# Pairing 768 instead of 1024 keys of the mixed heads in a graph attention kernel

## Chip, cores and metric

One core of a Trainium2 chip runs the whole program. The metric is device time in microseconds, lower is better. PE is TensorE's matmuls, PEld its weight loads, DVE VectorE, ACT ScalarE, POOL GpSimd, SP the engine that issues most DMAs.

## What is computed

A layer of graph convolution (x, 3327 nodes by 128) is followed by an attention layer over all pairs of nodes, in 128 heads of 8 components. The attention is where the time goes:

```python
q = (x @ Wq.T).reshape(d, n, h)      # d = 128 heads, n = 3327 nodes, h = 8
k = (x @ Wk.T).reshape(d, n, h)
v = (x @ Wv.T).reshape(d, n, h)
a = jnp.einsum('dnh,dmh->dnm', q, k) * scale
a = a + adj + adj
a = jax.nn.softmax(a, axis=2)
out = jnp.einsum('dnm,dmh->dnh', a, v)
out = out.reshape(n, h * d)
return out @ Wo.T
```

A layer norm of x + out closes it. adj has about five entries a row; the kernel takes the dense softmax without adj and adds the few neighbours of a node apart, on POOL.

## The kernel before

**Three passes over the same products.** Heads are worked in 32 groups of GH = 4, and the queries of a group in seven blocks of 512 (the last has 255). For each head and query the kernel needs (a) the largest product over all 3327 keys, so that exp can't overflow, (b) exp of every product less that maximum, (c) the sums of exp times v. Products come from PE as bf16 parts: query and key rows are split in three bf16 parts, 48 rows in all. The parts lie twice in the tiles k_st and q_st: rows 0 to 49 for (b), with two more rows that add the negative maximum, and rows 64 to 111 for (a).

**(a) is a stream of items.** `items_of` lists, for each row tile i of 128 queries, thirteen items; `max_item` (L544) works one: two matmuls of 512 keys (L553) into the two banks of a PSUM tile m of 1024 columns (pool ps_m, two buffers), then DVE takes the maximum of a row into a slot of mx (L573). Two of the four heads (MIXED = 0 and 2) save DVE work by pairs: of two keys a and b the larger product is half the sum plus the size of half the difference, s + |d|. The stage before stores half sums and half differences of neighbouring keys in kk_d (`mixed_keys`, `store_mixed`), and `load_group` (L282) puts them into the key tile of the mixed heads. PAIRED = 1024 keys of each mixed head are paired: 512 differences and 512 sums. A mixed head has three items:

- "size": a bank of 512 half differences and a bank of 512 plain keys. ACT writes the sizes of the first (Abs, L563) to the tile size; DVE takes the maximum of the second. The two read different banks of one tile, and the code says so with declare_no_dep.
- "sums": a bank of 512 half sums and a bank of 512 plain keys. DVE adds sizes and sums and keeps the maximum in one instruction (L567, tile larger, followed by a read of its accumulator), then takes the maximum of the plain bank.
- a plain item of 1024 keys.

The head next to it has three plain items. So the thirteen are size, sums, plain, three plain, again for heads 2 and 3, and one item of tails, the last 255 keys of all four heads.

**The order is written out by hand** (manual_schedule from L696). An iteration of the main loop (L735 to L772) takes the next item of the stream and interleaves it with (b) and (c) of a block that is 76 items behind. Its order of issue: the item's first matmul (L553), the first e_ps matmul (L751; ps_e has three buffers), the item's second matmul, the second e_ps matmul, exp of the first bank on ACT (L761, es<-e_ps), Abs if the item is a size item, exp of the second bank, the item's DVE instructions, and then four products with v (L719) of two iterations back. There are 10816 iterations and as many items. At the ends of a block some products are bunched in 512 columns, and o_sb (L728) is copied out.

**Beside it**: after a block's last item DVE reduces the slots of mx to nm (L516), POOL splits it in two bf16 parts, DVE transposes them (L529, tile turned), and SP sends them to the queries' extra rows. Every fourth iteration the generator `neighbours` issues a step of the neighbours' part: gathers and products on POOL, some maxima on DVE (L655 to L660), exponentials on ACT (L667). SP's loads of the next group's keys and next block's queries are cut in pieces, and one piece is started with every second item (`begin_next`).

Of the kernel before, what the change touches and what calls it, by code (L numbers as in the profile page):

```python
# [9 lines left out]
F32 = mybir.dt.float32  # L10
# [3 lines left out]
AF = mybir.ActivationFunctionType  # L14
ALU = mybir.AluOpType
AX = mybir.AxisListType
# [4 lines left out]
P = 128  # L21
N = 3327
# [6 lines left out]
NB = 512  # L29
# [6 lines left out]
PARTS = 3  # L36
# [7 lines left out]
LOWEST = -3.0e38  # L44
MW = 1024
# [4 lines left out]
LEAD = 38  # L50
TURN = 8
MIXED = (0, 2)
PAIRED = MW
SLOTS_MX = 5


def paired_from(head):

    return -head * N % (2 * D)
# [7 lines left out]
def gnn_layers(ctx: ExitStack, tc: tile.TileContext, x, adj, adjt, w_in, w_out, wq, wk, wv, wo, out):  # L67


    nc = tc.nc  # L70
# [19 lines left out]
    kk_d = dram.tile([2 * PARTS * H, G // 2], BF16, name="kk_d")  # L90
# [31 lines left out]
    with ExitStack() as c0:  # L122
# [4 lines left out]
        with ExitStack() as c1:  # L127
# [19 lines left out]
            rows = c1.enter_context(tc.tile_pool(name="rows", bufs=6))  # L147
# [76 lines left out]
            for t0 in range(0, NT, 2):  # L224
# [7 lines left out]
                    op=ALU.is_equal,  # L232
# [49 lines left out]
        def load_group(g):  # L282
            k = k_st[g % 2]
            v4 = load.tile([P, GH, NT, VW], F32, name="v4")
            heads = k_d[:, g * GH * N : g * GH * N + GH * N]
            pairs = []
            for slot, parts in KROWS:
                src = heads[: H * parts].rearrange("r (j n) -> r j n", j=GH)
                pairs.append((k[H * slot : H * slot + H * parts, :, :N], src))
                rows = slice(64 + H * slot, 64 + H * slot + H * parts)  # L290
                for j in range(GH):
                    if j not in MIXED:
                        pairs.append((k[rows, j, :N], src[:, j]))
                        continue
                    n0 = paired_from(g * GH + j)
                    at = ((g * GH + j) * N + n0) // 2
                    for s in range(2):
                        pairs.append(
                            (
                                k[rows, j, s * PAIRED // 2 : (s + 1) * PAIRED // 2],  # L300
                                kk_d.rearrange("(a d h) x -> d a h x", a=PARTS, d=2)[s, :parts, :, at : at + PAIRED // 2],
                            )
                        )
                    if n0:
                        pairs.append((k[rows, j, PAIRED : PAIRED + n0], src[:, j, :n0]))
                    pairs.append((k[rows, j, PAIRED + n0 : N], src[:, j, PAIRED + n0 :]))
            for j in range(GH):
                at = (g * GH + j) * N
                pairs.append((v4[:, j, :, :], v_d[at : at + NP, :].rearrange("(t p) w -> p t w", p=P)))
            coming[g] = pairs  # L310
            return k, v4
# [16 lines left out]
        def group_of(g):  # L328
            if g not in groups:
                groups[g] = load_group(g)  # L330
            return groups[g]
# [24 lines left out]
        with ExitStack() as c1:  # L356
# [18 lines left out]
            def store_mixed(t, sb):  # L375
                for head in range(HEADS):
                    if head % GH not in MIXED:
                        continue
                    first = (head * N + paired_from(head)) // (2 * D)
                    p0, p1 = max(first, t * P), min(first + PAIRED // (2 * D), (t + 1) * P)  # L380
                    while p0 < p1:
# [8 lines left out]
            for t in range(NT // 2):  # L390
# [5 lines left out]
                for s in range(2):  # L396
                    for name in ("wq", "wk", "wv"):
                        pr = ps_pr.tile([P, H * D], F32, name="pr")
                        rows = x1t[:, 2 * t * P : 2 * (t + 1) * P].rearrange("d (p s) -> d s p", s=2)[:, s]
# [43 lines left out]
    with c_att as c1:  # L443
        fixed = c1.enter_context(tc.tile_pool(name="fixed", bufs=1))
        q_pool.append(c1.enter_context(tc.tile_pool(name="q_pool", bufs=5)))
        work = c1.enter_context(tc.tile_pool(name="work", bufs=2))
# [10 lines left out]

        mxs = [fixed.tile([P, NB // P, GH, SLOTS_MX], F32, name=f"mx{i}") for i in range(2)]
        for mx in mxs:
            nc.vector.memset(mx, LOWEST)  # L460

        def items_of(mx, i):


            plain = {
                j: [([(j, c)], [(j, c + NB)], "all", [mx[:, i, j, c // MW : c // MW + 1]]) for c in range(0, 3 * MW, MW)]
                for j in range(GH)
            }
            for n, j in enumerate(MIXED):
                at = lambda slot: mx[:, i, j, slot : slot + 1]  # L470
                yield [(j, PAIRED // 2)], [(j, PAIRED)], "size", [at(1)]
                yield [(j, 0)], [(j, PAIRED + NB)], "sums", [at(0), at(3)]
                yield plain[j][2]
                yield from plain[j + 1]
            yield [(0, 3 * MW), (1, 3 * MW)], [(2, 3 * MW), (3, 3 * MW)], "tails", [mx[:, i, :, SLOTS_MX - 1]]

        def maxima():
            for g in range(NG):
                for b, (n0, w) in enumerate(BLOCKS):
                    ntl = -(-w // P)  # L480
                    k, _ = group_of(g)
                    q = queries_of(g, b)
                    begin_all(g)
                    begin_all((g, b))

                    if b == 2 and g + 1 < NG:
                        group_of(g + 1)
                    if b + 1 < len(BLOCKS) or g + 1 < NG:
                        queries_of(g + (b + 1) // len(BLOCKS), (b + 1) % len(BLOCKS))
                    mx = mxs[(g * len(BLOCKS) + b) % 2]  # L490
                    for i in range(ntl):
                        for n, item in enumerate(items_of(mx, i)):
                            turn()
                            if n % 2 or ntl < NB // P:
                                begin_next()
                            yield (k, q, i, *item)
                    late.append([1, lowest, (g, b, q, mx)])
            for _ in range(TURN + 4):
                turn()
                yield None  # L500
# [41 lines left out]
        sizes = []  # L542

        def max_item(item):  # L544

            k, q, i, *banks, kind, dst = item
            m = ps_m.tile([P, MW], F32, name="m")
            tail = N - 3 * MW
            for n, bank in enumerate(banks):
                width = NB if len(bank) == 1 else tail  # L550
                for x, (j, c0) in enumerate(bank):
                    at = n * NB + x * NB // 2
                    nc.tensor.matmul(  # L553
                        m[:, at : at + width],
                        q[64 : 64 + KR, j, i * P : (i + 1) * P],
                        k[64 : 64 + KR, j, c0 : c0 + width],
                        start=True,
                        stop=True,
                    )
                yield  # L560
            if kind == "size":
                sizes.append(work.tile([P, NB], F32, name="size"))
                taken = nc.scalar.activation(sizes[-1], m[:, :NB], AF.Abs)  # L563
            yield
            if kind == "sums":
                larger = work.tile([P, NB], F32, name="larger")
                nc.vector.tensor_tensor_reduce(  # L567
                    larger, sizes.pop(0), m[:, :NB], scale=1.0, scalar=LOWEST, op0=ALU.add, op1=ALU.max, accum_out=dst[0]
                )
            src = m if kind == "all" else m[:, NB:]  # L570
            if kind == "tails":
                src = m.rearrange("p (n c) -> p n c", n=GH)[:, :, :tail]
            reduced = nc.vector.tensor_reduce(dst[-1], src, axis=AX.X, op=ALU.max)  # L573
            if kind == "size":
                tc.declare_no_dep(reduced.ins, taken.ins, reason="they read two banks of one tile")
            yield
# [119 lines left out]
        with tc.manual_schedule(engines={ENG.PE, ENG.Activation, ENG.DVE, ENG.Pool, ENG.SP}):  # L696

            def next_item():
                item = next(stream, None)
                return max_item(item) if item is not None else iter(())  # L700
# [35 lines left out]
            for g in range(NG):  # L736
                for b, (n0, w) in enumerate(BLOCKS):
                    k, v4 = group_of(g)
                    q = queries_of(g, b)
                    per = 1 if w == NB else 2  # L740
                    for t in range(NT):
                        pt = P if t < NT - 1 else P - (NP - N)
                        e = []
                        for j0 in range(0, GH, 2 * per):
                            m = next_item()
# [23 lines left out]
                        size = NB // 2 if 0 < t < NT - 1 else NB  # L769
# [259 lines left out]
```

## Time and profile before

| | us |
|---|---|
| median of 3 runs | 13528.42 (13523.13 to 13529.55) |
| the profiled execution | 13508.75 |
| its span, first to last instruction | 13507.1 |
| main loop, first to last es instruction's start | 931.1 to 13264.1 |
| PE busy | 12886.6 (95%) |
| DVE busy | 12614.9 (93%) |
| ACT busy | 12708.6 (94%) |
| POOL busy | 5243.3 (39%) |

Each line of the profile's groups names line, engine, operation, the tile written and the tile read, the form and the count; then the busy time in us, the mean time of one in ns, and the idle time of the engine just before it with what ended it. A busy time is the union of the instructions' times, so it is less than count times mean where neighbours overlap. The listing in order of time gives start in us, length in us, engine, line and operation; equal neighbours are merged with a count, and brackets hold the idle time ahead. PEclk is the clock that was granted to TensorE, 1.00 in the main loop.

### The profile page before, as it was taken

Reading aid. Unit: us, or ns where it says so; the run is one execution under the profiler, and the core shown is the slowest. Engines: PE = TensorE matmul, PEld = TensorE weight load, DVE = VectorE, ACT = ScalarE, POOL = GpSimd, SP = SyncE. Lnnn points to the kernel's source line nnn. Section 1 sums busy time; section 2 is a strip of 40 time slices with the busy share of each in tenths; the row PEclk is TensorE's granted clock in tenths of the full one; section 3 lists DMA queues with packets and bytes.
Section 4 is the critical chain, followed back from the end, with each engine's and each line's share of the span. In section 5 each row is a group of like instructions: output and inputs, shape, how many; then the busy total and the mean of one; then the engine's idle time right before and its main releaser. Section 6 shows DMA issues by size and latency. Waiting matters only on the chain.

```text
span 13507.1 us, 323789 instructions
## 1 busy us (share of the span) xinstructions
PE 12886.6 (95%) x131844; PEld 3259.1 (24%) x131844; DVE 12614.9 (93%) x16015; ACT 12708.6 (94%) x24146; POOL 5243.3 (39%) x4554
## 2 busy tenths in 40 slices
PE   7669999999999999999999999999999999999996
PEld 3312222222222222222222222222222222222224
DVE  9779999999999999999999999999999999999996
ACT  6549999999999999999999999999999999999994
POOL 0310000004555555555545555555555555554100
PEclk9869999999999999999999999999999999999997
DMA  6753333333334443333334333444433334343203
GB/s 237 198 116 29 30 33 30 31 32 61 64 62 73 72 72 67 66 68 63 62 66 68 66 67 66 72 70 67 67 67 66 68 68 68 64 62 62 38 9 109
DMA packets 2618909, 929.93 MB, mean 69 GB/s; under 512 B 2261888, under 2 KB 2469896, under 8 KB 2610746
## 3 DMA queue, kind: packets, MB, share of 16 engines
q1 hardware_dynamic: 2485594, 399.03, 24.7%
q0 software_dynamic: 127920, 465.26, 12.5%
q10 hardware_dynamic: 3888, 44.82, 0.9%
q8 instruction: 1035, 16.96, 0.6%
q14 instruction: 472, 3.87, 0.1%
HBM read 786.21 MB, written 151.52 MB: 69 GB/s over the span
## 4 chain that ended last, share of the span: by engine, by line
PE 80%; DVE 10%; ACT 5%; DMA 2%; issue 2%; SPq 1%; POOL 0%; DVEq 0%; ACTq 0%; POOLq 0%
PE o L719 39%; PE m L553 35%; PE e_ps L751 5%; DVE mx L573 5%; ACT es L761 4%; DVE larger L567 1%; DMA q_d<-parts 1%; PE acc L190 1%; DVE top_at L200 1%; DVE top_w L199 1%; PE y L803 1%; ACT size L563 1%; SPq L340 0%; DVE parts L427 0%; ACT o_sb L728 0%
## 5 line engine op out<-in xcount | busy, mean ns | idle before, releaser
L761 ACT ACTIVATE es<-e_ps 128x512 f32<-128x512 f32 x21632 | 11442.9, 610 | 161.6 <-PE e_ps L751 115.8
L573 DVE TENSOR_REDUCE mx<-m 128x1 f32<-128x1024 f32 (+2 forms) x10816 | 10646.5, 1048 | 73.9 <-PE e_ps L751 40.8
L751 PE MATMUL e_ps<-q_st,k_st 50*128 50x512 bf16 (+1 forms) x23296 | 6814.4, 366 | 107.5 <-ACT es L761 101.2
L553 PE MATMUL m<-k_st,q_st 48*128 48x512 bf16 (+1 forms) x23296 | 6516.1, 367 | 145.4 <-DVE mx L573 84.0
L719 PE MATMUL o<-es,v 128*9 128x256 f32 (+1 forms) x83456 | 6623.3, 389 | 5.2 <-ACT o_sb L728 5.2
L553 PEld LDWEIGHTS <-q_st 48*128 48x128 bf16 x23296 | 1419.3, 94 | 5012.7 <-issue 4876.5
L719 PEld LDWEIGHTS o<-es,v 128*9 128x9 f32 x83456 | 1242.2, 88 | 4350.3 <-issue 4328.8
L522 POOL CAST two<-nm 128x16 bf16<-128x16 f32 (+1 forms) x224 | 44.1, 197 | 5754.8 <-DVE nm L516 5754.8
L567 DVE CUSTOM_DVE_ANT_0 larger<-size,m 128x512 f32<-128x512 f32 x1664 | 1142.8, 687 | 509.8 <-PE e_ps L751 471.8
L751 PEld LDWEIGHTS <-k_st 50*128 50x128 bf16 (+1 forms) x23296 | 1402.0, 95 | 214.6 <-issue 184.6
L563 ACT ACTIVATE size<-m 128x512 f32<-128x512 f32 x1664 | 985.7, 592 | 109.2 <-PE m L553 77.5
L639 POOL TENSOR_TENSOR prod<-qn,near_rows 128x1024 f32<-128x1024 f32 x416 | 987.3, 2373 | 27.9 <-DMA q_st<-q_d 12.0
L685 POOL TENSOR_TENSOR acc<-acc,prod 128x1024 f32<-128x1024 f32 x390 | 887.7, 2276 | 30.6
L684 POOL TENSOR_TENSOR prod<-near_rows,s 128x1024 f32<-128x1024 f32 x390 | 772.5, 1981 | 7.0
L641 POOL TENSOR_TENSOR half<-prod 128x512 f32<-128x512 f32 x416 | 530.1, 1274 | 32.6
L599 POOL DMA_INDIRECT near_rows<-kn_d,near x416 | 418.6, 1006 | 108.6 <-issue 51.4
L599 POOL DMA_INDIRECT near_rows<-vn_d,near x416 | 412.8, 992 | 61.4 <-issue 15.5
L190 PE MATMUL acc<-a_t,x 128*128 128x512 f32 (+1 forms) x728 | 309.6, 582 | 63.4 <-DMA a_t<-in_adj_dram 43.5
L668 POOL TENSOR_TENSOR s<-s,gain 128x2048 f32<-128x2048 f32 x26 | 93.9, 3611 | 692.2 <-ACT s L667 692.2
L643 POOL TENSOR_TENSOR quarter<-half 128x256 f32<-128x256 f32 x416 | 254.9, 613 | 32.6
L188 ACT ACTIVATE unread<-a_t 128x3327 bf16<-128x3327 f32 x52 | 155.0, 2980 | 103.9 <-PE acc L190 38.3
L190 PEld LDWEIGHTS acc<-a_t,x 128*128 128x128 f32 x728 | 140.0, 197 | 216.5 <-issue 172.6
(153 smaller groups left out, 3262.7 us busy)
## 6 DMA issues: line engine op xcount, KB each, us to landing
q_st<-q_d SPq DMA_DIRECT2D x2304, 32.0 KB
a_t<-in_adj_dram ACTq DMA_DIRECT2D x13, 1663.5 KB
a_t<-in_adj_dram SPq DMA_DIRECT2D x13, 1663.5 KB
a_t<-in_adjt_dram SPq DMA_DIRECT2D x13, 1663.5 KB
a_t<-in_adjt_dram ACTq DMA_DIRECT2D x13, 1663.5 KB
q_d<-parts SPq DMA_DIRECT2D x13, 1536.0 KB
k_d<-parts SPq DMA_DIRECT2D x13, 1536.0 KB
k_st<-k_d SPq DMA_DIRECT2D x32, 623.8 KB
```

The lines of the kernel that those rows point to most:

```text
L190: nc.tensor.matmul(acc[:, b, :w], x0[:, t, :], a_t[:, n0 : n0 + w], start=t == 0, stop=t == NT - 1)
L553: nc.tensor.matmul(m[:, at : at + width], q[64 : 64 + KR, j, i * P : (i + 1) * P], k[64 : 64 + KR, j, c0 : c0 + width], start=True, stop=True,
L563: taken = nc.scalar.activation(sizes[-1], m[:, :NB], AF.Abs)
L567: nc.vector.tensor_tensor_reduce(larger, sizes.pop(0), m[:, :NB], scale=1.0, scalar=LOWEST, op0=ALU.add, op1=ALU.max, accum_out=dst[0])
L573: reduced = nc.vector.tensor_reduce(dst[-1], src, axis=AX.X, op=ALU.max)
L599: nc.gpsimd.indirect_dma_start(rows.rearrange("p d h -> p (d h)"), None, table, bass.IndirectOffsetOnAxis(ap=near[:, t, i : i + 1], axis=0))
L639: nc.gpsimd.tensor_mul(prod, qn, kg)
L684: nc.gpsimd.tensor_mul(prod, vg, share)
L685: nc.gpsimd.tensor_add(acc[:, :, :H], acc[:, :, :H], prod)
L719: nc.tensor.matmul(o[32 * j : 32 * j + VW, c : c + w], v4[:pt, j, t, :], e[j][:pt, c : c + w], start=t == 0, stop=t == NT - 1,)
L751: nc.tensor.matmul(bank[:pt, j, :w], k[: KR + 2, j0 + y * per + j, t * P : t * P + pt], q[: KR + 2, j0 + y * per + j, :w], start=True, sto ...
L761: nc.scalar.activation(es[:pt, :, :w], bank[:pt, :, :w], AF.Exp, scale=2.0)
```

## The change

PAIRED falls from 1024 to 768 keys. The banks of half differences and half sums become 384 columns wide, and 128 plain keys fill each of them up to 512. The matmuls keep number and size. Abs and the larger instruction take 384 columns instead of 512. The sums item now has three DVE instructions: a maximum over the 128 plain keys that lie behind the differences in the size item's m (which is kept until then), the larger instruction over 384, and one maximum over 640 columns, the 128 plain keys behind the sums and the 512 of the second bank. mx gets a sixth slot. `load_group` loads one more piece for each mixed head and part, and `store_mixed` stores three partitions of pairs for each head instead of four; as it stores powers of two, each head has two stores instead of one.

```diff
--- before.py
+++ after.py
@@ -50,8 +50,9 @@
 LEAD = 38
 TURN = 8
 MIXED = (0, 2)
-PAIRED = MW
-SLOTS_MX = 5
+PAIRED = 768
+HALF = PAIRED // 2
+SLOTS_MX = 6
 
 
 def paired_from(head):
@@ -292,18 +293,21 @@
                     if j not in MIXED:
                         pairs.append((k[rows, j, :N], src[:, j]))
                         continue
+
                     n0 = paired_from(g * GH + j)
+                    n1 = n0 + PAIRED + NB - HALF
                     at = ((g * GH + j) * N + n0) // 2
-                    for s in range(2):
+                    for s, c0 in ((1, 0), (0, NB)):
                         pairs.append(
                             (
-                                k[rows, j, s * PAIRED // 2 : (s + 1) * PAIRED // 2],
-                                kk_d.rearrange("(a d h) x -> d a h x", a=PARTS, d=2)[s, :parts, :, at : at + PAIRED // 2],
+                                k[rows, j, c0 : c0 + HALF],
+                                kk_d.rearrange("(a d h) x -> d a h x", a=PARTS, d=2)[s, :parts, :, at : at + HALF],
                             )
                         )
+                    pairs.append((k[rows, j, HALF:NB], src[:, j, n0 + PAIRED : n1]))
                     if n0:
-                        pairs.append((k[rows, j, PAIRED : PAIRED + n0], src[:, j, :n0]))
-                    pairs.append((k[rows, j, PAIRED + n0 : N], src[:, j, PAIRED + n0 :]))
+                        pairs.append((k[rows, j, NB + HALF : NB + HALF + n0], src[:, j, :n0]))
+                    pairs.append((k[rows, j, NB + HALF + n0 : N], src[:, j, n1:]))
             for j in range(GH):
                 at = (g * GH + j) * N
                 pairs.append((v4[:, j, :, :], v_d[at : at + NP, :].rearrange("(t p) w -> p t w", p=P)))
@@ -468,8 +472,8 @@
             }
             for n, j in enumerate(MIXED):
                 at = lambda slot: mx[:, i, j, slot : slot + 1]
-                yield [(j, PAIRED // 2)], [(j, PAIRED)], "size", [at(1)]
-                yield [(j, 0)], [(j, PAIRED + NB)], "sums", [at(0), at(3)]
+                yield [(j, 0)], [(j, MW)], "size", [at(1)]
+                yield [(j, NB)], [(j, MW + NB)], "sums", [at(0), at(3), at(4)]
                 yield plain[j][2]
                 yield from plain[j + 1]
             yield [(0, 3 * MW), (1, 3 * MW)], [(2, 3 * MW), (3, 3 * MW)], "tails", [mx[:, i, :, SLOTS_MX - 1]]
@@ -559,18 +563,20 @@
                     )
                 yield
             if kind == "size":
-                sizes.append(work.tile([P, NB], F32, name="size"))
-                taken = nc.scalar.activation(sizes[-1], m[:, :NB], AF.Abs)
+                sizes.append((work.tile([P, HALF], F32, name="size"), m))
+                taken = nc.scalar.activation(sizes[-1][0], m[:, :HALF], AF.Abs)
             yield
             if kind == "sums":
-                larger = work.tile([P, NB], F32, name="larger")
+                size, m_size = sizes.pop(0)
+                nc.vector.tensor_reduce(dst[2], m_size[:, HALF:NB], axis=AX.X, op=ALU.max)
+                larger = work.tile([P, HALF], F32, name="larger")
                 nc.vector.tensor_tensor_reduce(
-                    larger, sizes.pop(0), m[:, :NB], scale=1.0, scalar=LOWEST, op0=ALU.add, op1=ALU.max, accum_out=dst[0]
+                    larger, size, m[:, :HALF], scale=1.0, scalar=LOWEST, op0=ALU.add, op1=ALU.max, accum_out=dst[0]
                 )
-            src = m if kind == "all" else m[:, NB:]
+            src = m if kind == "all" else m[:, NB:] if kind == "size" else m[:, HALF:]
             if kind == "tails":
                 src = m.rearrange("p (n c) -> p n c", n=GH)[:, :, :tail]
-            reduced = nc.vector.tensor_reduce(dst[-1], src, axis=AX.X, op=ALU.max)
+            reduced = nc.vector.tensor_reduce(dst[1] if kind == "sums" else dst[0], src, axis=AX.X, op=ALU.max)
             if kind == "size":
                 tc.declare_no_dep(reduced.ins, taken.ins, reason="they read two banks of one tile")
             yield
```

## Prediction

> **What bounds the kernel now.** I read the busy times of the steady stretch first, then the groups, the waits, and last the listing in order of time, where the limit shows. The stretch from 2000 to 12000 us:
>
> ```profile
> core 0: us, PE busy (x) PEld busy (x) DVE busy (x) ACT busy (x) POOL busy (x), PEclk, DMA share, GB/s
> 2000.00:12000.00 10000.00, 9842.30 (x105352) 2337.26 (x105348) 9531.83 (x11940) 9866.47 (x19146) 4768.28 (x4080) 1.00 0.39 63
> ```
>
> Three engines look full, ACT most. The chain and the groups (busy us, mean ns of one, idle before) say what they do:
>
> ```profile
> PE 80%; DVE 10%; ACT 5%; DMA 2%; issue 2%; SPq 1%; POOL 0%; DVEq 0%; ACTq 0%; POOLq 0%
> ...
> L761 ACT ACTIVATE es<-e_ps 128x512 f32<-128x512 f32 x21632 | 11442.9, 610 | 161.6 <-PE e_ps L751 115.8
> L573 DVE TENSOR_REDUCE mx<-m 128x1 f32<-128x1024 f32 (+2 forms) x10816 | 10646.5, 1048 | 73.9 <-PE e_ps L751 40.8
> ...
> L567 DVE CUSTOM_DVE_ANT_0 larger<-size,m 128x512 f32<-128x512 f32 x1664 | 1142.8, 687 | 509.8 <-PE e_ps L751 471.8
> ...
> L563 ACT ACTIVATE size<-m 128x512 f32<-128x512 f32 x1664 | 985.7, 592 | 109.2 <-PE m L553 77.5
> ```
>
> Busy time counts an instruction from its start to its last write, so neighbours overlap. What counts is the step from start to start. PE between a "size" item and the plain item two later:
>
> ```profile
> 6007.59 0.39 PE L553 MATMUL m<-k_st,q_st 48*128 48x512 bf16 x1
> ...
> 6008.12 0.62 PE L719 MATMUL o<-es,v 128*9 128x256 f32 x8
> 6008.68 0.39 PE L553 MATMUL m<-k_st,q_st 48*128 48x512 bf16 x1
> ...
> 6009.76 0.39 PE L553 MATMUL m<-k_st,q_st 48*128 48x512 bf16 x1
> ...
> 6009.99 0.38 PE L553 MATMUL m<-k_st,q_st 48*128 48x512 bf16 x1
> 6010.16 0.37 PE L751 MATMUL e_ps<-q_st,k_st 50*128 50x512 bf16 x1
> 6010.46 0.62 PE L719 MATMUL o<-es,v 128*9 128x256 f32 x8
> 6011.01 0.39 PE L553 MATMUL m<-k_st,q_st 48*128 48x512 bf16 x1
> ```
>
> An undisturbed iteration takes 1.087 us (6007.59, 6008.68, 6009.76). The third takes 1.25: its second e_ps matmul starts 0.17 us behind its m matmul, where the others start together. It wants the bank that es one item back must empty, and ACT is late because Abs came in between:
>
> ```profile
> 6008.04 0.60 ACT L761 ACTIVATE es<-e_ps 128x512 f32<-128x512 f32 x1
> 6008.54 0.59 ACT L563 ACTIVATE size<-m 128x512 f32<-128x512 f32 x1
> 6009.02 0.60 ACT L761 ACTIVATE es<-e_ps 128x512 f32<-128x512 f32 x1
> ```
>
> Abs holds ACT for 0.48 us (6008.54 to 6009.02). The next es starts at about 9.50, ends at 10.10, and PE goes on at 10.16. VectorE in the same stretch:
>
> ```profile
> 6008.33 0.68 DVE L573 TENSOR_REDUCE mx<-m 128x1 f32<-128x512 f32 x1
> 6009.42 0.69 DVE L567 CUSTOM_DVE_ANT_0 larger<-size,m 128x512 f32<-128x512 f32 x1 [0.42 <-PE e_ps L751]
> 6010.04 0.08 DVE L567 DVE_READ_ACCUMULATOR2_ANT mx<- 128x1 f32 x1
> 6010.04 0.68 DVE L573 TENSOR_REDUCE mx<-m 128x1 f32<-128x512 f32 x1
> ```
>
> DVE is free ahead of "larger": it waits for the sums' matmuls. In the list of waits this is DVE's only large one:
>
> ```profile
> DVE larger L567 <- PE e_ps L751: 384.4, 1181, 0.9
> ...
> PE m L553 <- DVE mx L573: 61.8, 215, 1.1
> ```
>
> Start to start, unheld, the trace has for DVE 1131 ns (1024 keys), 603 (512), 613 (larger); for ACT 477 (512, Abs as es). Thirteen items are nine wide reductions, four of 512 and two larger: 9 x 1.131 + 4 x 0.603 + 2 x 0.613 = 13.82 us of DVE. ACT: 28 x 0.477 = 13.36. PE: 13 x 1.087 = 14.13. The loop (first es 931 us, last 13264, 10816 iterations) takes 1.140 each, 14.82 per thirteen. So **PE sets the pace**, is held by ACT after each Abs, and DVE has 0.3 us to spare against PE.
>
> **What the Trainium skill says.** "Perfetto Trace Analysis", DVE / Act Engine Instruction: a profiled instruction runs from its start in the ALUs to the acknowledged write, and semaphore waits lie outside. The trace agrees: es lasts 597 ns and the next starts after 477. "ScalarE: Activation LUTs", What ACT_TABLE_LOAD costs: an ACTIVATE takes a fixed part plus 0.833 ns per element. The trace agrees: 1024 wide (L409) 1021 ns, 512 wide about 600, or 0.82 ns. "VectorE: DVE Perf Modes", the perf-mode tier table: tensor_reduce has only the 1x speed. The trace: (1131 - 603)/512 = 1.03 ns per key. "PSUM — Partial Sum Buffer", PSUM bank collisions raise a hardware error: two engines must be kept apart on one bank, reads too. Before, Abs and the reduction beside it read two banks and overlap (6008.33 and 6008.54); the new 128-key reduction shares Abs's bank, so it has to come after Abs. No run yet shows that wait.
>
> **The change part by part** (1664 mixed head tiles: 832 row tiles x 2).
>
> *Abs 512 to 384.* 128 x 0.83 = 107 ns less on ACT. All that follows on ACT moves up by it, so PE's hold of 166 ns becomes 59. At the ends of a block ACT is late as well (o_sb and Abs close together), so I count the same there. 1664 x 0.107 = **-178 us**, on the path.
>
> *Larger 512 to 384*, -128 x 1.04 = -133 ns; *last reduction 512 to 640*, +132 ns. Sum: nothing. Both lie behind the same wait as now.
>
> *A new 128-key reduction* ahead of larger. On the line of the other two sizes it costs 603 - 384 x 1.03 = 207 ns; the 128-wide maximum of L660 gives 209 to the next start. I take 0.20; added work can't cost less than nothing. Ends: 0.14 (a maximum over 80 values, L516, with nothing behind it that waits) and 0.32 (L516 to the next working start when a separate wait instruction follows). DVE rises to 13.82 + 2 x 0.20 = 14.22 per thirteen, 0.03 **above** PE's held pace of 14.13 + 0.06. Its cover is the wait: larger starts 907 ns (median) after the size reduction, of which 603 are work. 105 of the rest is a separate wait instruction in front of larger, which now waits for both ACT and PE. The new reduction takes over the wait for ACT, so I expect that instruction gone and data ready at 802. Work is 803. The cover is used up to the last nanosecond, in the median.
>
> *So what is late next is DVE.* Work that fell into that wait free now pushes PE: nm and turned (224 x (0.21 + 0.125) = 75 us) and the neighbours' maxima (52 + 26 of 0.60, 26 of 0.45, 26 of 0.21: 64 us). Of these 139 us I charge four tenths: part is already paid now (within a block, iterations other than the held ones average 1.097, not 1.087) and each block's start gives DVE time to catch up. **+60 us**, between 0 and 139.
>
> *The added wait for Abs.* Abs ends 623 ns after the size reduction starts, 107 less after the change: before the 603 at which DVE could start. Behind it on DVE wait larger, which needs Abs anyway, and PE's m of the plain item. That needs the bank about 0.3 us later than it is freed. I cost it at 0; where ACT is later (its 95th percentile is 846 ns) up to 0.14.
>
> *DMAs.* Three more key pieces per mixed head, six per group on SP, 43 instead of 37 in some 48 slots open before the last block: hidden. In the stage before, 128 stores of mixed keys instead of 65, with three quarters of the bytes: SP spends 65 x 2.3 us on them; a quarter less is -37, and 63 more of the shortest issue (0.285) +18. SP is not what that stage waits for, so I take 0, between -19 and +18. The 76 items ahead of the loop are paced by DVE: 12 x 0.2 = **+2 us**. nm reads six slots: nothing.
>
> Sum: -178 + 60 + 2 = **-116 us** on the profiled execution, 13508.75 (span 13507.1 and 1.65 around it): 13393. The median of the runs, 13528.42, lies 0.15% higher; the same share off gives **13412**.
>
> **The rivals.** (1) *Give-back*: the separate wait stays in front of larger, so that larger begins as late as now and the lag carried on grows by about 0.1 us per tile; DVE stalls PE on m where ACT did. Per tile -107 + 107: 13528, no change. For it: two engines to wait for. Against: the reduction after larger carries no wait of its own, so waits already seen are dropped. (2) *Slower*: DVE is the bound and the new reduction costs its upper end, as a short instruction that must first wait for ACT. Each 0.1 us beyond the cover costs 166 us; 0.11 x 1664 = +183, -116 + 183 = +67: 13595. It decides from about 0.27 us. For it: DVE's 14.22 per thirteen is already past PE. Against: L660's 0.21. (3) *Nothing given back*: DVE catches up at every block's start: 13350. That the change doesn't do what it says is excluded: the sizes are written out.
>
> **How the numbers follow.** Likeliest with (3): 0.68, its own range 13350 to 13460. Give-back 0.14. Slower 0.18. The range 13345 to 13545 takes in give-back and leaves out most of slower. About 0.2% (27 us) can be told from no change: faster 0.68, same 0.14, slower 0.18.
>
> **What would show it.** Right: Abs at about 485 ns, iterations after the sums at about 1.15 instead of 1.25, the wait ahead of larger nearly gone, a new reduction stepping 0.20. Wrong: waits of m for DVE growing from 62 us to several hundred (give-back); a step of the new reduction above 0.27, or idle time ahead of it for ACT (slower).

## Result, and the profile after

| | before | after |
|---|---|---|
| median of the runs, us | 13528.99 | 13367.55 |
| the profiled execution, us | 13508.75 | 13363.41 |
| span, us | 13507.1 | 13361.7 |
| first to last es instruction | 931.1 to 13264.1 | 925.2 to 13119.3 |

The ratio is 0.9888 (0.9868 to 0.9908): 1.1% faster, some 150 us. (The medians lie 161 us apart; one of the four runs after took 13408.8 us, and the ratio is what the text goes by.) In the profiled executions the main loop gave 139 us of 145, the stages before it 6.

The busy times of the steady stretch after the change:

```profile
core 0: us, PE busy (x) PEld busy (x) DVE busy (x) ACT busy (x) POOL busy (x), PEclk, DMA share, GB/s
2000.00:12000.00 10000.00, 9843.07 (x106530) 2377.35 (x106528) 9860.24 (x13434) 9831.61 (x19359) 4816.44 (x4114) 1.00 0.39 64
```

DVE has gone from 95.3% to 98.6% busy and is now the fullest engine, ACT has fallen a little, PE is where it was; yet more is done in the same time (105352 matmuls before, 106530 after). The chain and the groups of the page:

```profile
PE 79%; DVE 14%; ACT 3%; DMA 2%; issue 1%; SPq 1%; POOL 0%; DVEq 0%; ACTq 0%; POOLq 0%
...
L767 ACT ACTIVATE es<-e_ps 128x512 f32<-128x512 f32 x21632 | 11447.8, 612 | 197.4 <-PE e_ps L757 126.5
L579 DVE TENSOR_REDUCE mx<-m 128x1 f32<-128x1024 f32 (+3 forms) x10816 | 10874.1, 1071 | 77.2 <-PE e_ps L757 40.2
...
L573 DVE CUSTOM_DVE_ANT_0 larger<-size,m 128x384 f32<-128x384 f32 x1664 | 914.6, 550 | 66.0 <-PE e_ps L757 60.9
L567 ACT ACTIVATE size<-m 128x384 f32<-128x384 f32 x1664 | 809.6, 487 | 106.7 <-PE m L557 46.7
...
L571 DVE TENSOR_REDUCE mx<-m 128x1 f32<-128x128 f32 x1664 | 472.6, 284 | 27.0 <-ACT size L567 10.3
```

Two groups carry the story. Abs lasts 487 ns instead of 592. And DVE's idle time ahead of larger has fallen from 509.8 to 66.0 us, with the new reduction (472.6 us) in its place. The share of ACT on the chain went from 5% to 3%, that of DVE from 10% to 14%.

PE in the listing in order of time, from a sums item over the plain item behind it:

```profile
6589.80 0.39 PE L557 MATMUL m<-k_st,q_st 48*128 48x512 bf16 x1
...
6590.89 0.39 PE L557 MATMUL m<-k_st,q_st 48*128 48x512 bf16 x1
...
6591.11 0.38 PE L557 MATMUL m<-k_st,q_st 48*128 48x512 bf16 x1
6591.18 0.37 PE L757 MATMUL e_ps<-q_st,k_st 50*128 50x512 bf16 x1
6591.48 0.62 PE L725 MATMUL o<-es,v 128*9 128x256 f32 x8
6592.03 0.39 PE L557 MATMUL m<-k_st,q_st 48*128 48x512 bf16 x1
```

The second e_ps matmul is now 0.07 us behind its m matmul (6591.11 and 6591.18) where it was 0.17 behind, and the iteration takes 1.14 us (6590.89 to 6592.03) instead of 1.25. ACT and DVE in the same stretch:

```profile
6589.66 0.48 ACT L567 ACTIVATE size<-m 128x384 f32<-128x384 f32 x1
6590.03 1.10 ACT L767 ACTIVATE es<-e_ps 128x512 f32<-128x512 f32 x2
```

```profile
6589.59 0.68 DVE L579 TENSOR_REDUCE mx<-m 128x1 f32<-128x512 f32 x1
6590.19 0.28 DVE L571 TENSOR_REDUCE mx<-m 128x1 f32<-128x128 f32 x1
6590.44 0.56 DVE L573 CUSTOM_DVE_ANT_0 larger<-size,m 128x384 f32<-128x384 f32 x1
```

Abs holds ACT for 0.37 us (6589.66 to 6590.03) instead of 0.48. The new reduction starts at 6590.19, 0.60 us behind the size reduction, which is as soon as DVE can; Abs has just ended, at 6590.14. Larger starts 0.41 us behind the sums' second m matmul (6590.03 to 6590.44). Before, that distance was 0.52 us (6008.90 to 6009.42):

```profile
6008.90 0.38 PE L553 MATMUL m<-k_st,q_st 48*128 48x512 bf16 x1
```

Over all 1664 the medians are 522 ns before and 415 after.

The waits of 2000 to 12000 us (total us, times, longest) hold a warning about reading them:

```profile
PEld L557 <- DVE mx L579: 710.9, 1306, 1.4
...
PE e_ps L757 <- ACT es L767: 65.3, 176, 0.6
PE m L557 <- DVE mx L579: 64.9, 218, 1.6
DVE larger L573 <- PE e_ps L757: 49.8, 130, 1.4
```

The weight loads of m wait 711 us for DVE, before 18. It looks as if DVE held PE up. It doesn't. The loads wait while PE is still busy with the products of the iteration before, and most of the same idle time was put down to "issue" (3882 us before, 3314 after). The wait of PE's own queue for DVE is 65 us, as before (62). The run with DVE's part alone, below, settles it: its loads wait 704 us for DVE as well, and it takes as long as the kernel before.

### The profile page after: what moved, and what is told of

It reads as the page before. It is cut to its first block, busy times and chain, and to the rows that moved or that the text cites. A ratio compares the mean times of both kernels' runs of the same rounds, so it can differ in the third digit from the quotient of the medians.

```text
span 13361.7 us, 325240 instructions
## 1 busy us (share of the span) xinstructions
PE 12748.4 (95%) x131844; PEld 3270.1 (24%) x131844; DVE 12885.2 (96%) x17679; ACT 12532.3 (94%) x24146; POOL 5245.4 (39%) x4554
## 4 chain that ended last, share of the span: by engine, by line
PE 79%; DVE 14%; ACT 3%; DMA 2%; issue 1%; SPq 1%; POOL 0%; DVEq 0%; ACTq 0%; POOLq 0%
PE o L725 39%; PE m L557 35%; DVE mx L579 9%; PE e_ps L757 4%; ACT es L767 2%; DVE larger L573 1%; PE acc L191 1%; DMA q_d<-parts 1%; DVE top_at L201 1%; DVE top_w L200 1%; PE y L809 1%; DVE mx L571 0%; SPq L344 0%; ACT o_sb L734 0%; ACT size L567 0%
## 5 line engine op out<-in xcount | busy, mean ns | idle before, releaser
L579 DVE TENSOR_REDUCE mx<-m 128x1 f32<-128x1024 f32 (+3 forms) x10816 | 10874.1, 1071 | 77.2 <-PE e_ps L757 40.2
L757 PE MATMUL e_ps<-q_st,k_st 50*128 50x512 bf16 (+1 forms) x23296 | 6661.1, 366 | 87.0 <-ACT es L767 78.8
L573 DVE CUSTOM_DVE_ANT_0 larger<-size,m 128x384 f32<-128x384 f32 x1664 | 914.6, 550 | 66.0 <-PE e_ps L757 60.9
L567 ACT ACTIVATE size<-m 128x384 f32<-128x384 f32 x1664 | 809.6, 487 | 106.7 <-PE m L557 46.7
L571 DVE TENSOR_REDUCE mx<-m 128x1 f32<-128x128 f32 x1664 | 472.6, 284 | 27.0 <-ACT size L567 10.3
```

Source lines behind the costliest of these rows:

```text
L567: taken = nc.scalar.activation(sizes[-1][0], m[:, :HALF], AF.Abs)
L573: nc.vector.tensor_tensor_reduce(larger, size, m[:, :HALF], scale=1.0, scalar=LOWEST, op0=ALU.add, op1=ALU.max, accum_out=dst[0])
L579: reduced = nc.vector.tensor_reduce(dst[1] if kind == "sums" else dst[0], src, axis=AX.X, op=ALU.max)
L757: nc.tensor.matmul(bank[:pt, j, :w], k[: KR + 2, j0 + y * per + j, t * P : t * P + pt], q[: KR + 2, j0 + y * per + j, :w], start=True, sto ...
```

## Experiments

Theory A: what counts is ACT's time between a size item and the es two banks later; DVE's added work lies in a wait. Rival B: the gain came from DVE, whose larger is shorter and starts earlier. Ratios are to the kernel before, run on the same chip. The diffs are cut to the lines that matter; "steps" are times from one start to the next.

### Each engine's part alone

ACT's part, put into the kernel before (two fixed size tiles, zeroed once):

```diff
-taken = nc.scalar.activation(sizes[-1], m[:, :NB], AF.Abs)
+taken = nc.scalar.activation(sizes[-1][:, :384], m[:, :384], AF.Abs)
```

> The kernel before (1024 keys in pairs, DVE's instructions as before) with Abs on 384 of the 512 differences; the sizes of the other 128 are left at zero, so 128 differences are left out of the maximum. ACT's part of the change alone. Theory A (what counts is ACT's time between a size item and the es two banks later): 107 ns for each of 1664 mixed tiles, nothing given back since DVE has its old work: 13528 - 178 = 13350. Rival B (the gain came from DVE: larger starts 105 ns earlier behind its matmuls and is shorter): no change, 13528.

Measured: 0.9917 (0.9904 to 0.993), 13408 us. Faster, so B alone is out; but 112 us, not 178. DVE's part, the kernel after with Abs over the whole bank:

```diff
-taken = nc.scalar.activation(sizes[-1][0], m[:, :HALF], AF.Abs)
+taken = nc.scalar.activation(sizes[-1][0], m[:, :NB], AF.Abs)
```

> The kernel after with Abs over the whole bank of 512 again (larger still takes 384 of it). DVE's part of the change alone. Theory A: ACT holds PE as before and DVE has 0.2 us more for each mixed tile, most of it inside the wait ahead of larger: 13530 to 13580. Rival B: nearly the whole gain stays, 13370 to 13400.

Measured: 0.9992 (0.9984 to 1.0). Nothing gained and, against my expectation, nothing lost: 0.2 us of new DVE work for each mixed tile was free. ACT still holds PE here: the iterations after the sums take 1.253 us (median), as before. The two parts together give 1.12%, the parts alone 0.83 and 0.08. The intervals leave room for a plain sum, but they hint that the parts help each other, which neither A nor B says; the next runs show it.

### Without the new reduction, and with it twice

```diff
-nc.vector.tensor_reduce(dst[2], m_size[:, HALF:NB], axis=AX.X, op=ALU.max)
```

> The kernel after without the new 128-key reduction (128 keys of each mixed head are left out of the maximum). Theory A: what the added DVE work cost comes back and no more, 25 to 45 us below the kernel after: about 13325 to 13350. A rival in which DVE is the bound of the kernel after: 0.2 us for each of 1664 tiles less whatever PE then sets, 13250 or below.

Measured: 0.992 (0.9907 to 0.9933), 13409 us. The sign was wrong: **leaving DVE work out made the kernel slower** than the kernel after (the intervals just touch at 0.991; the traces below agree), back to the time of Abs alone shortened. Its group for larger, and that of the run with Abs alone, one page each:

```profile
L572 DVE CUSTOM_DVE_ANT_0 larger<-size,m 128x384 f32<-128x384 f32 x1664 | 921.7, 554 | 431.0 <-PE e_ps L756 407.1
```

```profile
L572 DVE CUSTOM_DVE_ANT_0 larger<-size,m 128x512 f32<-128x512 f32 x1664 | 1143.7, 687 | 434.4 <-PE e_ps L756 406.4
```

The idle time ahead of larger is back (431 us and 434), and in both larger starts 520 ns (median) behind the sums' second m matmul, not 415. Without the new reduction larger must again wait for ACT and for PE. The trace has the wait for PE as an instruction of its own in front of all 1664. PE in the run with Abs alone shortened, from the last plain item over the tails to the next row tile's size and sums items:

```profile
6599.87 0.39 PE L557 MATMUL m<-k_st,q_st 48*128 48x512 bf16 x1
...
6601.00 0.27 PE L557 MATMUL m<-k_st,q_st 48*128 48x255 bf16 x1
...
6602.13 0.37 PE L557 MATMUL m<-k_st,q_st 48*128 48x512 bf16 x1
...
6603.26 0.37 PE L557 MATMUL m<-k_st,q_st 48*128 48x512 bf16 x1
...
6604.35 0.39 PE L557 MATMUL m<-k_st,q_st 48*128 48x512 bf16 x1
```

Three iterations in a row take 1.13 us: DVE's step for 1024 keys, not PE's 1.087. With ACT out of the way PE runs into DVE, which is late because larger starts late. In this run five of thirteen iterations do so (medians 1.124 to 1.130). The iterations after the sums, in turn, take 1.09 us: PE comes to them so late that ACT no longer holds it.

The other way, the reduction done twice:

```diff
+for d in dst[2:]:
+    nc.vector.tensor_reduce(d, m_size[:, HALF:NB], axis=AX.X, op=ALU.max)
```

> The kernel after with the 128-key reduction done twice, the second into a seventh slot. Theory A: the cover ahead of larger is used up after the first (larger starts 843 ns after the size reduction in the median, work is 796), DVE's work per thirteen items goes from 14.22 to 14.62 us, past PE's 14.25: 150 to 300 us above the kernel after, 13520 to 13670. If there were cover left: under 30 us.

Measured: 1.0048 (1.0036 to 1.0061), 13575 us: 1.6 points, some 216 us above the kernel after. The second 0.2 us costs 0.13 us for each mixed tile. The cover takes one such instruction and about a third of a second.

### The wait handed over

So I formed theory A2: ACT's 107 ns let PE go, and DVE can follow only if larger starts earlier, which the change gets from any instruction ahead of it that takes over the wait for ACT. To the kernel with Abs alone shortened I added an instruction that does nothing else:

```diff
+size = sizes.pop(0)
+nc.vector.tensor_reduce(seen, size[:, :2], axis=AX.X, op=ALU.max)
 larger = work.tile([P, NB], F32, name="larger")
```

> The run with Abs alone shortened (e1_abs_384: 128 differences left out of the maximum), and a tiny DVE instruction ahead of larger that reads two columns of the tile size, so that it takes over the wait for ACT and larger waits for PE alone. In that run five of thirteen iterations took 1.125 to 1.130 us, DVE's step. Theory A2 (two parts: ACT's 107 ns let PE go, and larger then must start earlier behind its matmuls, which the change gets from the new reduction taking over the wait for ACT): ratio to before 0.986 to 0.9885, as the kernel after or a little below, since the tiny instruction is shorter than 128 keys. Rival B2 (what the shortened Abs lacked is something else that the change does, such as the shorter larger or another arrangement of the keys): as that run, 0.9917.

Measured: 0.9865 (0.985 to 0.9879), 13339 us. The whole 178 us are there, within the interval (1.35% of 13517 is 182). PE of this run, from the last but one plain item over the tails to the next row tile's size item:

```profile
6564.15 0.39 PE L559 MATMUL m<-k_st,q_st 48*128 48x512 bf16 x1
...
6565.24 0.39 PE L559 MATMUL m<-k_st,q_st 48*128 48x512 bf16 x1
...
6566.33 0.28 PE L559 MATMUL m<-k_st,q_st 48*128 48x255 bf16 x1
...
6567.42 0.39 PE L559 MATMUL m<-k_st,q_st 48*128 48x512 bf16 x1
```

The last plain item and the tails step 1.09 us again. Over the whole run so do four of the five slow kinds of iteration (medians); the fifth, the first size item of a row tile, stays at 1.127, where it was in the kernel before (1.126). Larger starts 413 ns behind its matmul. An added instruction took 0.5% off. The same instruction in the kernel before, with nothing else changed:

> The kernel before with nothing but the tiny DVE instruction ahead of larger that takes over the wait for ACT. Theory A2: larger starts some 105 ns earlier, but PE is held by ACT in the iteration after, as with DVE's part of the change alone: ratio 0.997 to 1.001. A rival in which the earlier larger is a gain of its own: 0.995 or below.

Measured: 0.9987 (0.998 to 0.9993), 13504 us, inside what A2 gives. Larger starts 414 ns behind its matmul, and the iterations after the sums still take 1.254 us. Where ACT holds PE, an earlier larger is worth almost nothing.

### ACT's time in another place, and more of it

A small Abs between two SBUF tiles of 64 columns behind each Abs of the kernel after:

```diff
+nc.scalar.activation(idle_out, idle_in, AF.Abs)
```

> The kernel after with one more ACT instruction behind each Abs (64 columns, from one small tile to another, nobody waits for it), some 100 ns by the line of 512 (477) and 384 (370). Theory A: ACT's time is what counts, wherever it is spent between a size item and the es after: the gain is gone, ratio 0.998 to 1.003. A rival in which Abs counts because it frees m's bank earlier: as the kernel after, about 0.989.

Measured: 1.0037 (1.0023 to 1.005), 13565 us, some 200 us above the kernel after and a little past what theory A gave. The filler steps 146 ns, not 100; 1664 x 0.146 = 243 us, of which four fifths reach the end. Nobody waits for it and it touches no PSUM, so it is ACT's time that counts and not when m's bank is freed. Abs on 256 columns in the kernel before:

```diff
-taken = nc.scalar.activation(sizes[-1], m[:, :NB], AF.Abs)
+taken = nc.scalar.activation(sizes[-1][:, :256], m[:, :256], AF.Abs)
```

> As e1_abs_384 with Abs on 256 columns (256 differences left out of the maximum), ACT 214 ns shorter for each mixed tile instead of 107. Theory A2: inside a block DVE's pace already holds five of thirteen iterations, so only the ends of blocks, where ACT is late, gain further: 10 to 50 us below e1_abs_384, ratio 0.988 to 0.991. If ACT's time alone counted: 166 ns of hold for each of 1664 tiles, 276 us, ratio 0.98.

Measured: 0.9896 (0.9882 to 0.9911), 13378 us, 30 us below Abs on 384 (the intervals overlap a little). The second 107 ns bring about a quarter of what the first did: DVE has the pace.

### Other sizes

Only PAIRED changes, and the partitions of pairs that are stored, rounded up:

```diff
-PAIRED = 768
+PAIRED = 896
+STORED = 1024
...
-p0, p1 = max(first, t * P), min(first + PAIRED // (2 * D), (t + 1) * P)
+p0, p1 = max(first, t * P), min(first + STORED // (2 * D), (t + 1) * P)
```

> The kernel after with 896 keys in pairs: banks of 448 half differences or sums and 64 plain keys. The whole reference is computed. Abs is 53 ns shorter than before instead of 107, DVE's added work about 0.13 us instead of 0.20. Theory A2: PE's hold after the sums falls from 166 to 113, 88 us off, nearly nothing given back: ratio 0.993 to 0.995. If DVE's added work were what limits the kernel after, this would be as fast or faster: 0.988 or below.

Measured: 0.9948 (0.9934 to 0.9962), 13443 us.

> The kernel after with 640 keys in pairs: banks of 320 and 192 plain keys. The whole reference is computed. Abs is 160 ns shorter than before, DVE has 0.26 us more than before for each mixed tile. Theory A2: PE's hold is down to 6 ns, but DVE's 14.34 us for thirteen items are past PE's 14.14, so DVE sets the pace: 30 to 110 us slower than the kernel after, ratio 0.990 to 0.997. If ACT's time alone counted: 0.981 to 0.984.

With PAIRED = 640 and STORED = 768, measured: 0.992 (0.9906 to 0.9934), 13421 us. Its size items and tails step 1.13 us, DVE's step again. So of 1024, 896, 768 and 640 paired keys, 768 is the fastest: more pairs leave ACT in the way, fewer give DVE more than it can hide. Against 640 the lead is small: the intervals just touch, and two of its five runs took 13386 and 13390 us. Only the run with Abs on 384 columns and the wait handed over, which leaves keys out of the maximum, had a lower ratio than the kernel after, and those intervals overlap.

## Why the prediction was right

The direction, the mechanism and the range were right; the gain came out at 151 us against 116.

- *Abs, -107 ns each, -178 us.* Right. Abs steps 370 ns instead of 477, the iterations after the sums take 1.148 us instead of 1.253 (medians), and the run with the wait handed over shows the full 178 where DVE's cost is close to nothing. In the trace of the loop the iterations after the sums gained 182 us together.
- *Larger and the last reduction cancel.* Right: 613 to 479, 603 to 736 ns.
- *The new reduction, 0.20 us, in the cover ahead of larger.* Right in size (198 ns to the next start) and in place. DVE's part alone cost nothing, and a second one cost 216 us.
- *The separate wait instruction goes and larger is ready at 802.* The effect is right (522 to 415 ns behind the matmul, 107 ns earlier), the detail is not: 1162 of 1664 larger instructions still have a wait instruction in front. It waits for DVE's own earlier result instead of PE, so it is over before PE's data come. I treated this as part of the cover. It carries about a third of the gain: 1.12% with it against 0.80% without the new reduction, and 1.35% against 0.83% where the tiny instruction did the same.
- *Give-back, +60 us.* Too large; this is the mis-sized term. In the trace the loop gained 139 of 178, so 39. (The ratio of the kernel after stands 0.23 points, about 30 us, above that of the run with the tiny instruction, which agrees, though these intervals overlap.) Two slips made DVE look tighter than it was. The 907 ns from the size reduction to larger is the lower quartile of the kernel before; its median over all 1664 is 944, so the cover was not used up to the last nanosecond, but had some 36 to spare. And thirteen iterations hold two mixed tiles, so PE's held pace is 14.13 + 2 x 0.059 = 14.25, not 14.19, and DVE's 14.22 lies 0.03 below it, not above. Where the give-back fell fits the reason given for it: of 42 us that the iterations other than those after the sums lost, some 25 lie in the first row tile of a block, where the trace has nm and turned on DVE. By kind, 17 lie at the sums items, 13 at the last plain items of a head and 9 at the size items.
- *The added wait for Abs, 0.* The wait is there, but not always. In the median the new reduction starts 598 ns after the size reduction, as soon as DVE can. In about a third of the cases (579 of 1664) it starts right behind Abs's end, 32 ns at the least. It is hidden, as DVE's part alone shows: there Abs ends later, the reduction starts at 751 in the median, and nothing is lost.
- *The stages before, +2.* The loop started 6 us earlier. Fewer bytes of mixed keys is a reason that fits; it wasn't tried.
- *Rival (1), give-back because larger starts late,* is a real mechanism, and the runs without the reduction show it. Its price was too high: with it 0.8% of gain is left, not none. *Rival (2), DVE the bound,* is what a second reduction brings about, 0.5% slower than before. The kernel after stands close to it: 98.6% busy.

## What to carry to other kernels

When three engines are full in turn, find which one holds PE in which iteration, and price a change there; shortening the holder shows the next one at once, and the gain stops where that one's pace begins. A wait that an instruction has to make for two engines can be handed to an earlier instruction on the same queue, even to one that costs time. What that is worth depends on who holds PE: 0.5% here where DVE did, 0.1% where ACT did. Work that is added inside a wait is free up to the wait's length; beyond it, it costs most of its time (0.13 of 0.2 us here).

## What was not expected

- An instruction of DVE that waits for two engines, with the wait for PE in an instruction of its own, started 520 to 522 ns (medians) behind the start of the matmul it waits for; with the wait for ACT made by an earlier instruction, 413 to 415 ns. It was worth 0.5% of this kernel once ACT was out of the way.
- A 64-column Abs from SBUF to SBUF stepped 146 ns on ACT; the line through 477 ns (512 columns) and 370 ns (384) from PSUM gives 103.
